# Turning a unit's maxima by four VectorE block transposes in place of one TensorE transpose

## The chip, the core and the metric

The kernel runs on one core of a Trainium2 chip. The core has a matrix engine (TensorE, "PE" in the profile, whose weight loads are listed apart as "PEld"), three engines for elementwise work (VectorE "DVE", ScalarE "ACT", GpSimd "POOL") and SyncE ("SP"), which here only issues transfers. Each engine runs its own list of instructions in order and waits on semaphores for the others. The metric is the time of one execution in microseconds (us) on the device; the kernel before takes 3283.42 us in the median of three runs.

## The reference

One transformer block with normalisation ahead of each half, on an input `x` of 2 x 1024 tokens of width 1024, with 32 heads of 32 and a gated network of inner width 2752, all in float32:

```python
x = x + attn(layernorm(x))
x = x + ffn(layernorm(x))

def attn(x):
    qkv = (x @ attn_qkvw + attn_qkvb).reshape(B, S, 3, HEADS, hd)
    q, k, v = ...                                  # each (B, HEADS, S, hd)
    scores = einsum('bhqd,bhkd->bhqk', q, k) / sqrt(hd)
    ctx = einsum('bhqk,bhkd->bhqd', softmax(scores, axis=-1), v)
    return ctx.transpose(0, 2, 1, 3).reshape(B, S, H) @ attn_ow + attn_ob

def ffn(x):
    return (silu(x @ W_gate.T) * (x @ W_up.T)) @ W_down.T
```

The part that matters here is the softmax: before the exponential, the maximum over all keys is subtracted for each head and each query.

## The kernel before, in words

The work is cut in four blocks: two batches by two halves of 512 query tokens. A block is done in this order: projections of q, k and v (L370, L432), attention, the output projection (`po`, L780), the second normalisation with its transposes (L258), the gated network (products `p`, L922, and `pd`, L1071 and L998; both by seven products on sums of quarters in place of eight, the sums of weights being made once on POOL, L1184).

Attention is cut in 64 units, 16 a block, each of two heads. A unit's scores are 8 tiles (`kt`) of 128 keys by 2 x 512 queries, made two at a time by `scores` (L510) into a PSUM tag "s" with two buffers. ScalarE copies each tile to SBUF (L529) and VectorE takes the running elementwise maximum `top` over the tiles (L526). When the last tile is through, `maximum` brings the 128 partitions of `top` to one value for each column:

- `half(s)`, twice (due 4600 and 6400 after the last scores): VectorE transposes 512 columns of `top` in blocks of 32x32 into `m` (L549) and takes the maximum over each block's rows (L550) into 16 columns of `part`. After it, partition 32a+i, column b of `part` holds the maximum of column 32b+i over the a-th group of 32 partitions. `part` is one tile of 128x128, of which only 32 columns are ever written; it is set to 0 at the start (L463).
- `turn` (due 10500): TensorE transposes all of `part` into a PSUM tile `top` of the tag "lin" (L564), and VectorE reduces the four groups of its first 32 partitions to `neg`, negated (L565).
- `neg` (32x32) is written to memory by SyncE (L570, due 12000) and read back by all 128 partitions into `m` (L573, due 14500).

Later steps add `m` to each tile of scores (`less_maximum`, L580, on POOL, and on VectorE for a quarter of the tiles of the first block), take the exponential on ScalarE (L589), add pairs of tiles (L603, on VectorE and POOL) and multiply with the values on TensorE (`acc`, L618).

The PSUM tag "lin" has three buffers, used in turn by every projection, every transpose of L258, the products of the network, and the `top` of L564. A buffer is free again when VectorE or ScalarE has read it: for `pd` that is L1084 (added to `x`), for `p` the small operations of L936 to L949, for `po` L792.

The order of instructions is written by the program, not by a scheduler. `Emitter.run` walks two lists: `fill`, which holds the projections and the network, with a cost in nanoseconds for each matmul (`MM4` = 855), and `paced`, which holds the attention's steps as evenly spaced beats. A clock is advanced by each step's cost. `em.later(delay, fn)` puts a step off until that clock has passed the present value by `delay`; it is then emitted at once, on whichever engine it names. So a due time sets the place of an instruction in its engine's list, not the moment at which it runs.

Of the kernel before, what the change touches and what calls it, by code (L numbers as in the profile page):

```python
# [9 lines left out]
F32 = mybir.dt.float32  # L10
F32R = mybir.dt.float32r
AF = mybir.ActivationFunctionType
ALU = mybir.AluOpType
AX = mybir.AxisListType

P = 128
HEADS = 32
HD = 32
# [112 lines left out]
def preln_block_kernel(  # L131
# [14 lines left out]
    nc = tc.nc  # L146
# [11 lines left out]
    HPG = P // HD  # L158
# [8 lines left out]
    const = ctx.enter_context(tc.tile_pool(name="const", bufs=1))  # L167
# [29 lines left out]
    def lps(name, shape=(P, NH)):  # L197
        return psum.tile(list(shape), F32, tag="lin", bufs=3, name=name)

    def small(shape, tag, bufs, name):  # L200
        return const.tile(shape, F32, tag=tag, bufs=bufs, name=name)

    ident = const.tile([P, P], F32, tag="ident", name="ident")
# [25 lines left out]
    em = Emitter()  # L229
# [229 lines left out]
    NQ = NH // 2  # L459


    part = const.tile([P, P], F32, tag="part", name="part")
    nc.vector.memset(part, 0.0)  # L463

    class Unit:

# [75 lines left out]
        def maximum(self):  # L542

            n = HD // NS
            self.m = att.tile([P, S], F32, tag="m", bufs=2, name=f"m_{self.name}")

            def half(s):
                cols = slice(s * NH, (s + 1) * NH)
                nc.vector.transpose(self.m[:, cols], self.top[:, cols])  # L549
                nc.vector.tensor_reduce(  # L550
                    part[:, s * n : (s + 1) * n],
                    self.m[:, cols].rearrange("p (b j) -> p b j", j=HD),
                    AX.X,
                    ALU.max,
                )

            for s in range(NS):
                em.later(4600.0 + 1800.0 * s, lambda s=s: half(s))
            d2 = dram.tile([S], F32, tag="d2", bufs=3, name=f"d2_{self.name}")
            neg = small([HD, HD], "neg", 1, f"neg_{self.name}")  # L560

            def turn():
                pt = lps(f"top_{self.name}", (P, P))
                nc.tensor.transpose(pt, part, ident)  # L564
                nc.vector.tensor_reduce(  # L565
                    neg, pt[:HD, :].rearrange("b (a i) -> b i a", i=HD), AX.X, ALU.max, negate=True
                )

            em.later(10500.0, turn)
            em.later(12000.0, lambda: nc.sync.dma_start(d2.rearrange("(b i) -> b i", i=HD), neg))  # L570
            em.later(
                14500.0,
                lambda: nc.sync.dma_start(self.m, d2.partition_broadcast(P)),  # L573
                ("max", self.n),
            )
# [777 lines left out]
```

## Time and profile before

| what | us |
|---|---|
| median of three runs | 3283.42 (3279.31 to 3285.41) |
| profiled execution | 3281.96 |
| its span, first to last instruction | 3280.2 |
| TensorE's granted clock, mean over the span | 0.994 of full |
| VectorE's L526, the running maximum, busy | 545.4 in 448 instructions |
| POOL's L580, subtraction of the maximum, busy | 1180.8 in 480 |
| TensorE's L922, products `p`, busy | 1091.3 in 4704 |
| TensorE's L1071, products `pd`, busy (its larger group) | 442.3 in 960 |

A group of the profile is one line's instructions on one engine: "out<-in" names the tiles by the program's names, "x64" the number, then the busy time in us, the mean of one in ns, and how long the engine stood idle just before them and what ended that. A float32 matmul shows as two records, a transpose as one. A wait "A <- B" is idle time of A ended by B. In a table of stretches of time, each engine has its busy time and count, then come the granted clock, the share in which the DMA engines were busy, and GB/s.

### The profile page before, as it was taken

How to read it: one execution, taken by the hardware profiler on the slowest of the kernel's cores; microseconds unless marked ns; L12 is line 12 of the kernel's file. 1: busy time of each engine (PE TensorE's matmuls, PEld its weight loads, DVE VectorE, ACT ScalarE, POOL GpSimd, SP SyncE). 2: the span in 40 equal slices, each digit the busy share in tenths (PEclk: the TensorE clock that was granted, in tenths of full speed). 3: DMA queues.
4: the chain of work that ended last, by engine and by line, in shares of the span. 5: the costliest groups of instructions: out<-in, count | busy, mean ns of one | idle time of the engine just before them, and what ended most of it. 6: DMA issues, size and time to landing. Idle time of an engine off the chain costs nothing. (4 is left out here: it accounts for less than half of the span.)

```text
span 3280.2 us, 43732 instructions
## 1 busy us (share of the span) xinstructions
PE 3217.5 (98%) x16320; PEld 1801.1 (55%) x16320; DVE 1920.4 (59%) x2478; ACT 1431.2 (44%) x1570; POOL 1758.6 (54%) x871
## 2 busy tenths in 40 slices
PE   8999999999999999999999999989999999999999
PEld 4444444444347655663466556634655566477775
DVE  2265676666356766666666666676666664344334
ACT  2244554444455545563655455545555554010000
POOL 0267776876676655568665555667765665200000
PEclk9999999999999999999999999999999999999999
DMA  4556766655534445446344444463444444544442
GB/s 155 171 184 193 226 192 203 200 180 161 158 99 135 142 151 146 146 146 200 107 142 145 139 141 137 145 192 110 137 145 146 146 138 140 184 151 153 153 152 97
DMA packets 337826, 507.29 MB, mean 155 GB/s; under 512 B 105424, under 2 KB 122064, under 8 KB 337616
## 3 DMA queue, kind: packets, MB, share of 16 engines
q1 hardware_dynamic: 281424, 405.91, 40.3%
q10 hardware_dynamic: 56192, 98.60, 9.8%
q8 instruction: 130, 2.13, 0.3%
q14 instruction: 80, 0.66, 0.1%
HBM read 429.14 MB, written 75.24 MB: 154 GB/s over the span
## 5 line engine op out<-in xcount | busy, mean ns | idle before, releaser
L580 POOL TENSOR_TENSOR p<-p,m 128x1024 f32<-128x1024 f32 x480 | 1180.8, 2483 | 13.6 <-DMA m<-d 13.4
L529 ACT COPY p<-s 128x1024 f32<-128x1024 f32 x512 | 516.7, 1011 | 872.1 <-DVE top L526 664.5
L526 DVE TENSOR_TENSOR top<-s,top 128x1024 f32<-128x1024 f32 x384 | 468.1, 1219 | 289.0 <-PE s L510 280.0
L589 ACT ACTIVATE p<-p 128x1024 f32<-128x1024 f32 x512 | 532.2, 1057 | 234.7 <-POOL p L580 206.8
L922 PE MATMUL p<-sum,m 128*128 128x256 f32 x2688 | 617.8, 383 | 4.9 <-DVE sum L904 3.3
L603 POOL TENSOR_TENSOR p<-p,p 128x1024 f32<-128x1024 f32 x96 | 227.2, 2367 | 658.9 <-ACT p L589 598.3
L922 PEld LDWEIGHTS p<-sum,m 128*128 128x128 f32 x2688 | 503.2, 190 | 124.7 <-issue 43.0
L922 PE MATMUL p<-xn2T,m 128*128 128x256 f32 x2016 | 473.5, 384 | 1.9 <-ACT gate L934 1.3
L370 PE MATMUL pq<-xnT,wqk 128*128 128x512 f32 x1024 | 463.7, 601 | 0.0
L1071 PE MATMUL pd<-wp,h 128*128 128x512 f32 x960 | 442.3, 607 | 8.3 <-DVE x L1084 6.4
L922 PEld LDWEIGHTS p<-xn2T,m 128*128 128x128 f32 x2016 | 378.2, 191 | 98.5 <-issue 45.4
L603 DVE TENSOR_TENSOR p<-p,p 128x1024 f32<-128x1024 f32 x192 | 306.2, 1595 | 134.1 <-ACT p L589 134.0
L370 PEld LDWEIGHTS pq<-xnT,wqk 128*128 128x128 f32 x1024 | 187.2, 190 | 252.8 <-issue 249.0
L1071 PEld LDWEIGHTS pd<-wp,h 128*128 128x128 f32 x960 | 179.3, 193 | 242.5 <-issue 203.4
L510 PE MATMUL s<-q,k 32*128 32x512 f32 x2048 | 300.8, 645 | 7.1 <-ACT p L529 7.0
L1084 DVE TENSOR_TENSOR x<-pd,x 128x512 f32<-128x512 f32 x360 | 236.9, 681 | 86.8 <-PE pd L1071 86.7
L618 PE MATMUL acc<-p,vals 128*32 128x256 f32 x4096 | 266.0, 383 | 1.8 <-DVE p L603 1.8
L1184 POOL TENSOR_TENSOR ws<-raw 128x512 f32<-128x512 f32 x62 | 93.7, 1512 | 299.9 <-DMA raw<-in_w_gu 170.5
L432 PE MATMUL pvv<-wv,xnT 128*128 128x512 f32 x512 | 233.3, 600 | 1.5 <-ACT xnT L266 1.5
L780 PE MATMUL po<-wo,ctx 128*128 128x512 f32 x512 | 234.6, 607 | 0.0
L618 PEld LDWEIGHTS acc<-p,vals 128*32 128x32 f32 x4096 | 120.1, 110 | 143.6 <-issue 70.2
L950 ACT ACTIVATE gate<-gate 128x512 f32<-128x512 f32 x84 | 52.9, 630 | 278.4 <-DVE gate L949 278.0
(96 smaller groups left out, 2451.3 us busy)
## 6 DMA issues: line engine op xcount, KB each, us to landing
m<-dws SPq DMA_DIRECT2D x336, 256.0 KB
m<-in_w_gu SPq DMA_DIRECT2D x252, 256.0 KB
wp<-ddn SPq DMA_DIRECT2D x160, 256.0 KB
m<-d SPq DMA_DIRECT2D x64, 512.0 KB
wp<-in_w_dn SPq DMA_DIRECT2D x120, 256.0 KB
raw<-in_w_gu ACTq DMA_DIRECT2D x84, 256.0 KB
dws<-ws ACTq DMA_DIRECT2D x84, 256.0 KB
x<-in_x SPq DMA_DIRECT2D x32, 512.0 KB
```

The costliest lines, as they stand in the source:

```text
L370: nc.tensor.matmul(ps, wqk[b, g, w, hk][:, k, :], xnT[b, s][:, kc, :], start=(kc == 0), stop=(kc == KC - 1),)
L510: nc.tensor.matmul(ps[a][:, h * NH : (h + 1) * NH], self.k[rows, i * P : (i + 1) * P], self.q[rows, :], start=True, stop=True,)
L526: nc.vector.tensor_tensor(self.top, s, self.p[0] if kt == 1 else self.top, ALU.max)
L529: nc.scalar.copy(self.p[kt], s)
L580: eng.tensor_tensor(p, p, self.m, ALU.add)
L589: nc.scalar.activation(self.p[kt], self.p[kt], AF.Exp, scale=SCALE)
L603: eng.tensor_tensor(self.p[kt], self.p[kt], self.p[kt - back], ALU.add)
L618: nc.tensor.matmul(self.acc[j * HD : (j + 1) * HD, c : c + NQ], w(h), self.p[kt][:, q0 : q0 + NQ], start=start, stop=stop, skip_group_chec ...
L780: nc.tensor.matmul(st["ps"], ctxT[b, blk][:, g, t * P : (t + 1) * P], st["w"][hf, g], start=(g == 0), stop=(g == G - 1),)
L922: nc.tensor.matmul(ps, mats[c, n][:, kc, :], rhs, start=(kc == 0), stop=(kc == hk - 1),)
L1071: nc.tensor.matmul(st["pd"], lefts[n](pi)[:, j, t * P : (t + 1) * P], st["wp", pi, n, j], start=(j == 0), stop=(j == PART // 2 - 1),)
L1084: nc.vector.tensor_tensor(xs, st["pd"], xs, op)
```

## The change

`part` shrinks from 128x128 to the 32 columns that are written, and is no longer set to 0. In `turn`, TensorE's transpose into PSUM goes; VectorE instead transposes each of the four 32x32 groups of `part` into its place in a new SBUF tile `turned` (32 partitions, 4 x 32), and the reduction reads that. `turn` is due at 8200 instead of 10500. The reduction's result, its write and its read back, and their due times, are the same.

```diff
-    part = const.tile([P, P], F32, tag="part", name="part")
-    nc.vector.memset(part, 0.0)
+    part = const.tile([P, HD], F32, tag="part", name="part")
...
+            turned = small([HD, HPG, HD], "turned", 1, f"turned_{self.name}")
+
             def turn():
-                pt = lps(f"top_{self.name}", (P, P))
-                nc.tensor.transpose(pt, part, ident)
+                for a in range(HPG):
+                    nc.vector.transpose(turned[:, a, :], part[a * HD : (a + 1) * HD, :])
                 nc.vector.tensor_reduce(
-                    neg, pt[:HD, :].rearrange("b (a i) -> b i a", i=HD), AX.X, ALU.max, negate=True
+                    neg, turned.rearrange("b a i -> b i a"), AX.X, ALU.max, negate=True
                 )
 
-            em.later(10500.0, turn)
+            em.later(8200.0, turn)
```

In the built program, the lists of TensorE (apart from the 64 transposes), ScalarE, POOL and SyncE are the same as before, instruction for instruction. On VectorE, the four transposes and the reduction stand directly behind the second `part` of L550 or up to three instructions later; before, the reduction stood one to four instructions behind it in all but five units.

## The prediction

> **What bounds the kernel now.** First the busy shares, to see which engine sets the time.
>
> ```profile
> PE 3217.5 (98%) x16320; PEld 1801.1 (55%) x16320; DVE 1920.4 (59%) x2478; ACT 1431.2 (44%) x1570; POOL 1758.6 (54%) x871
> ```
>
> TensorE (PE) is busy for 98% of the span of 3280.2 us, and the next engine, VectorE (DVE), for 59%. So an edit is worth what it takes from PE's own work, or from the 62.7 us (3280.2 - 3217.5) in which PE stood still; work moved to DVE costs only where DVE is late for PE. Second, the transpose that the change removes, by its line, L564.
>
> ```profile
> L564 PEld LDWEIGHTS top<-ident,part x64: 137/140/183, 126.7 to 2730.8; 128*128 128x128 f32 x64
> L564 PE MATMUL top<-ident,part x64: 272/273/474, 127.2 to 2731.1; 128*128 128x128 f32 x64
> ...
>   DVE part L550: 37.4, 22
> ...
>   DVE neg L565: 38.4, 22
> ```
>
> There are 64, one a unit. PE and its weight load together stood idle 37.4 us for `part` just before it, and in turn DVE's next step, `neg`, stood idle 38.4 us for it: a ping-pong between two engines that both run their queues in order. Third, PE's own waits.
>
> ```profile
> PE top L564 <- DVE part L550: 16.1, 10, 3.0
> PE pt_a L258 <- ACT x L247: 10.2, 4, 7.8
> PE pd L1071 <- DVE x L1084: 7.1, 12, 1.4
> ```
>
> The largest wait of all that PE has is the one that the change takes away.
>
> **The change part by part.** *a) The 64 transposes on PE.* A record lasts 273 ns, but matmuls are pipelined, so its price is how much later the next matmul starts. Where nothing waits, the timeline gives it:
>
> ```profile
> 2728.47 2.75 PE L922 MATMUL p<-xn2T,m 128*128 128x256 f32 x12
> ...
> 2731.06 0.27 PE L564 MATMUL top<-ident,part 128*128 128x128 f32 x1
> ...
> 2731.17 2.75 PE L922 MATMUL p<-xn2T,m 128*128 128x256 f32 x12
> ```
>
> The next matmul starts 0.11 us after it (2731.17 - 2731.06); read at 45 undisturbed places it is 0.109. 64 x 0.109 = 7.0 us, all on the path. The weight load (140 ns) lies under the matmul before.
>
> *b) PE's wait for `part`.* At 19 of the 64 places the start of the matmul in front of the transpose and that of the one behind it lie further apart than their usual distance (0.216 us after L922, 0.429 after L1071, 0.52 after the scores) plus 0.109. Summed over the timeline this excess is 28.0 us; the largest are 3.8 at 2031, 3.3 at 982, 3.1 at 1821, 3.0 at 2203 and 2.7 at 1534. How much comes back depends on what PE needs next. One place:
>
> ```profile
> 1817.97 1.28 DVE L1084 TENSOR_TENSOR x<-pd,x 128x512 f32<-128x512 f32 x2
> 1819.17 0.70 DVE L549 STREAM_TRANSPOSE m<-top 128x512 f32<-128x512 f32 x1
> 1819.90 0.69 DVE L550 TENSOR_REDUCE part<-m 128x16 f32<-128x512 f32 x1
> 1820.51 1.28 DVE L1084 TENSOR_TENSOR x<-pd,x 128x512 f32<-128x512 f32 x2
> ...
> 1824.04 0.27 DVE L565 TENSOR_REDUCE neg<-top 32x32 f32<-32x128 f32 x1
> ```
>
> ```profile
> 1817.47 1.14 PE L510 MATMUL s<-q,k 32*128 32x512 f32 x8
> 1820.64 0.33 PE L564 MATMUL top<-ident,part 128*128 128x128 f32 x1 [2.03 <-DVE part L550]
> 1821.84 5.12 PE L1071 MATMUL pd<-wp,h 128*128 128x512 f32 x8 [0.87 <-DVE x L1084]
> ```
>
> PE ends the scores at 1818.61, stands until 1820.64 for `part`, and then 0.87 us more, since its next product needs one of the three `lin` PSUM buffers and the transpose took the one that came free first. Without the transpose the product takes that one, free at 1819.25 (1817.97 + 1.28), so it could start 2.59 us earlier (1821.84 - 1819.25) of the 3.1 lost. I read this slack (start of a product less the end of the eviction three products before, transposes not counted) at all 19 places for the next four products: where it is the smaller, it replaces the wait. That leaves 23.8 of 28.0 us.
>
> *c) DVE's new work.* Four block transposes of 32x32 and the reduction, now out of SBUF, replace one reduction. No 32x32 transpose is in the trace; the nearest rows are
>
> ```profile
> L549 DVE STREAM_TRANSPOSE m<-top 128x512 f32<-128x512 f32 x128 | 89.9, 702 | 1.8
> L550 DVE TENSOR_REDUCE part<-m 128x16 f32<-128x512 f32 x128 | 87.8, 686 | 4.4
> ...
> L565 DVE TENSOR_REDUCE neg<-top 32x32 f32<-32x128 f32 x64 | 17.4, 272 | 38.6 <-PE top L564 38.4
> ...
> L243 DVE RECIPROCAL rstd_f<-sd_f 128x1 f32<-128x1 f32 x16 | 2.6, 164 | 10.3 <-ACT sd_f L241 10.3
> ```
>
> The two reductions give (686 - 272) / (512 - 128) = 1.08 ns an element above 134 ns, so 32 elements are 168 ns, and with the 16 ns by which a transpose exceeds a reduction of 512, about 0.18 us. The bounds are 0.044 (702 x 32 / 512, no fixed part) and 0.70 (no saving for a small one); 0.18 is nearest to the one-element operation's 0.164. Four are 0.72, the reduction 0.27, with one gap for dependent steps (0.03 after L549 above) 1.0 us a unit, against 0.27. Over the span DVE gains 64 x 0.75 = 48 us of work and loses 38.4 of waiting.
>
> DVE instructions that start back to back overlap: two L1084 of 0.68 take 1.28. The Trainium skill ("VectorE: DVE Perf Modes", section "Two Vector instructions with no wait between them") holds an instruction until the earlier ones have finished if its input starts in another quadrant of partitions than the last one's, as these four do; by it there is no overlap, as I took it; with overlap of 0.08 each a unit would cost 0.3 us less, at most 19 x 0.3 = 6 us of this sum. No row here shows it.
>
> *d) What is queued behind.* The steps are emitted earlier (due 8200 instead of 10500), so DVE runs them ahead of one to three instructions that stood between `part` and `neg`: in 63 units the add of L603, in some the evictions L1084 or L936 to L952. These come up to 1.0 us later, and PE waits for the evictions. The slack behind the transpose is 1.9 us or more at nearly every undisturbed unit (2.8 is usual in L922 stretches; over 12 before 880 us), so 1.0 is hidden there by PE's next products; without that cover it would be up to 46 x 1.0 us (the units from 890 us on). At the 19 places I take the full 1.0 from the slack: 17 us of b) stay. The scores' PSUM (7 us or more of slack at the first scores after the transpose in most units) and the add's users (median 16 us) are clear. On SyncE the write of `neg` (L570) keeps its place and due time; in 28 units it waited for `neg`, and loads queue behind it, so earlier can only help. POOL and ACT issue what they did. The memset of `part` (165 ns, at the start) is beside PE's wait for the first input.
>
> *e) The clock.* Behind the longest of these waits the granted clock is halved:
>
> ```profile
> 1821.32:1824.73 3.41, 2.89 (x4) 1.34 (x5) 3.25 (x6) 0.00 (x0) 0.00 (x0) 0.50 0.02 7
> ...
> 2203.61:2207.03 3.42, 3.42 (x10) 0.91 (x7) 1.93 (x3) 1.01 (x1) 3.22 (x1) 0.50 0.94 264
> ```
>
> The column with 0.50 is the clock. There are nine such stretches between 800 and 2300 us, and six begin in this wait or within 2.2 us behind its end (982, 1534, 1821, 1947, 2033, 2203; waits of 1.6 to 3.0 us). In those six, the steps between matmuls of one line are longer than usual by 8.5 us in all. With d) some 1 to 2 us of wait remains at three of the six, so I take 5 us (bounds 0 and 8.5). The Trainium skill ("TensorE: Matmul & The Clock Gate", section "HAM oscillation — how this bites in real kernels") asks only that idle gaps stay below about 3.4 us; by that none of these waits would lower the clock and the forecast would be 5 us longer. The trace disagrees: 1.62 us before 1946.9 was enough.
>
> *Sum.* 7.0 + 17 + 5 = 29 us. The profiled execution took 3281.96 us (span 3280.2 and 1.8 around it), 1.46 below the median of 3283.42, so 3253 for such an execution and **3254** on the median's scale.
>
> **The rivals.** *The wait only moves.* DVE is late for reasons of its own (between 1816.6 and 1824.5 it has no idle time), and PE waits at the next eviction instead. For it: weight loads of L1071 wait 34.5 us, 52 times, for L1084. Against: the slack of 1.9 to 2.6 us that the freed buffer gives. Then only a) remains: 3283.4 - 7.0 = 3276.
>
> *DVE becomes the limit: slower.* If a 32x32 transpose costs what L549 does, the turn is 4 x 0.70 + 0.27 = 3.1 us, and evictions behind it come 1.2 us past a slack of 1.9 in the 46 units from 890 us on: 55 us lost, against 7.0 and some 7 of the waits whose slack exceeds 3.1: 3283 + 41 = 3324. It decides from about 2.3 us a turn (46 x 0.4 = 18 us lost, against 7 and about 11), half a microsecond a transpose. Against: one-element and 12-element operations at 164 to 209 ns. In this sense the Trainium skill speaks against the change: "VectorE: DVE Perf Modes", section "Rules for kernel authors", gives a 128x128 transpose to TensorE and only a 32x32 one to DVE, and here four of the latter replace one of the former; the removed step needed only 32 columns of it, and by that rule's other row DVE is the right place.
>
> *Nothing comes of it.* What PE saves returns as waits for another chain, such as ACT's copies of the scores (L529; PE waited 7.0 us for them, and two halved stretches stand behind such waits): 3283. Against: the median slack of the scores' buffers, 5.5 us.
>
> **How the numbers follow.** Forecast (gain of 17 to 43 us, 3240 to 3266) 0.66; the wait moves 0.14; nothing 0.07; slower 0.09; a larger gain, by halved stretches vanishing elsewhere too, 0.04. The upper bound of the gain is 7.0 + 28.0 + 8.5 = 43.5, or 3240, and 2 for the scatter of single times gives the low end, 3238. The high end takes in the moved wait (3276) and 3 us of late evictions: 3279. A change under 0.2% (6.6 us) can't be told from none. Faster: 0.66 + 0.04 + two thirds of 0.14 = 0.79; within: the rest and 0.07, 0.11; slower 0.10.
>
> **What would show it.** a) No `top` record on PE, 64 matmuls fewer. b) PE idle falls from 62.7 to below 45 us, and the products behind 1818 and 2028 start some 1.5 to 2.6 us earlier after the scores. c) 32x32 transposes of 0.15 to 0.22 us, DVE busy near 1970 us, `neg` without idle time before it. d) Waits of PE and of weight loads for L1084 not above the present 7.1 and 34.5 us by more than 5. e) Halved stretches at 1534, 2203 and 982 gone or shorter. Transposes above 0.5 us, or L1084 in the place of `part` among PE's waits, would make the forecast wrong.

## The result, and the profile after

The changed kernel took 3267.21 us in the median of four executions, beside 3284.39 us for the kernel before: a ratio of 0.9954 (95% interval 0.9941 to 0.9967). Two later repeats, beside their own runs of the kernel before, gave ratios of 0.9950 (0.9938 to 0.9962) and 0.9953 (0.9940 to 0.9966). So it is faster by some 0.48% (by the mean of the three ratios, 0.9952), 16 us; 29 were forecast. The profiled execution was one of its fastest, 3264.24 us with a span of 3262.5.

The busy shares of the changed kernel, as in the first fence of the prediction:

```profile
PE 3206.8 (98%) x16256; PEld 1792.5 (55%) x16256; DVE 1999.2 (61%) x2733; ACT 1432.7 (44%) x1570; POOL 1767.8 (54%) x871
```

PE has its 64 records fewer, but it still stands still for 55.7 us (3262.5 - 3206.8), against 62.7. DVE's busy time grew by 79 us. The new steps, by their lines (least, median and longest in ns):

```profile
L566 DVE STREAM_TRANSPOSE turned<-part x256: 189/199/204, 122.6 to 2711.4; 32x32 f32<-32x32 f32 x128
```

```profile
L567 DVE TENSOR_REDUCE neg<-turned x64: 355/364/381, 123.5 to 2711.7; 32x32 f32<-32x128 f32 x64
```

Nothing waits before either of them. PE's own waits, longest first (total, times, longest):

```profile
PE s L509 <- ACT p L528: 10.5, 5, 3.9
PE pt_a L258 <- ACT x L247: 10.1, 4, 7.8
PE pd L1073 <- DVE x L1086: 9.9, 13, 1.9
PE acc L620 <- DVE p L605: 5.4, 3, 2.1
```

The wait for `part` is gone. In its place are longer waits for three things that other engines make: ACT's copies of the scores, DVE's evictions of `pd` (7.1 us before), and DVE's adds of the probabilities, which the products with the values (`acc`) read. The copies and the adds in the kernel before:

```profile
PE s L510 <- ACT p L529: 7.0, 5, 2.6
...
PE acc L618 <- DVE p L603: 1.8, 2, 1.5
```

The lines of the changed kernel are shifted by up to two: L1073 is L1071 of before, L605 is L603.

At the place that the prediction worked through, 1821 us before, the changed kernel does what was expected:

```profile
1812.34 1.28 DVE L1086 TENSOR_TENSOR x<-pd,x 128x512 f32<-128x512 f32 x2
1813.53 0.70 DVE L548 STREAM_TRANSPOSE m<-top 128x512 f32<-128x512 f32 x1
1814.27 0.69 DVE L549 TENSOR_REDUCE part<-m 128x16 f32<-128x512 f32 x1
...
1816.66 0.84 DVE L566 STREAM_TRANSPOSE turned<-part 32x32 f32<-32x32 f32 x4
1817.53 0.36 DVE L567 TENSOR_REDUCE neg<-turned 32x32 f32<-32x128 f32 x1
```

```profile
1811.81 1.14 PE L509 MATMUL s<-q,k 32*128 32x512 f32 x8
1813.67 1.98 PE L1073 MATMUL pd<-wp,h 128*128 128x512 f32 x4 [0.72 <-DVE x L1086]
```

The product starts 1.86 us after the scores' first record (1813.67 - 1811.81), where it was 4.37 us before (1821.84 - 1817.47): 2.51 us earlier, of 2.59 read from the buffers. In two more traces of the changed kernel it is 1.91 and 2.49.

**Where the gain is, and where it went.** Apart from the 64 transposes, the matmuls of both kernels are the same and in the same order, so each can be matched with itself, and the step from one to the next compared. Three sums come out: at the 19 places where PE had waited in the trace of before, at the other 45 places of the removed transpose, and everywhere else (us, positive is gained, against the profiled execution of before).

| profiled execution | 19 places | other 45 | elsewhere | in all |
|---|---|---|---|---|
| changed kernel, first | 26.7 | 5.3 | -14.3 | 17.7 |
| changed kernel, second (`again`) | 27.6 | 5.3 | -24.1 | 8.8 |
| changed kernel, third (`base`) | 26.8 | 5.3 | -19.4 | 12.7 |
| no block transposes (`no_blocks`) | 28.4 | 5.3 | -7.9 | 25.9 |
| no turn at all (`no_turn`) | 28.9 | 5.3 | -4.2 | 30.0 |

What was to be earned at the places of the transpose was earned, nearly all of it. Between 14 and 24 us were given back elsewhere. The last two rows are experiments, described below. The steps elsewhere can be split by the matmul that came later (us, the changed kernel as the mean of its three traces):

| steps elsewhere to | changed kernel | `no_turn` |
|---|---|---|
| scores (PE waits there for ACT's copies) | -5.7 | -6.1 |
| products with the values (for DVE's adds) | -6.3 | -2.5 |
| `pd` (for DVE's evictions) | -4.0 | +0.9 |
| any matmul while the clock is halved in either trace | -1.9 | +2.4 |
| all others | -1.3 | +1.0 |

So of the 15 us between the two columns 13 stand at the adds, the evictions and the clock. The loss at the scores is there without VectorE's turn too, so the turn does not explain it; from trace to trace it is 3.3 to 7.9 us, and what makes ACT's copies come late was not tried.

One place of the second row, 4 to 6 us behind a place where 2.67 us were gained (1534 us before):

```profile
1527.50 10.31 POOL L582 TENSOR_TENSOR p<-p,m 128x1024 f32<-128x1024 f32 x4
...
1531.61 1.07 PE L620 MATMUL acc<-p,vals 128*32 128x256 f32 x16
1531.87 0.84 DVE L566 STREAM_TRANSPOSE turned<-part 32x32 f32<-32x32 f32 x4
...
1532.75 0.38 DVE L567 TENSOR_REDUCE neg<-turned 32x32 f32<-32x128 f32 x1
...
1533.06 2.53 DVE L605 TENSOR_TENSOR p<-p,p 128x1024 f32<-128x1024 f32 x1
...
1535.64 0.64 PE L620 MATMUL acc<-p,vals 128*32 128x256 f32 x8 [2.10 <-DVE p L605]
```

The same add before, and the products of which the second half read it:

```profile
1533.45 1.49 DVE L603 TENSOR_TENSOR p<-p,p 128x1024 f32<-128x1024 f32 x1
...
1538.90 1.04 PE L618 MATMUL acc<-p,vals 128*32 128x256 f32 x16
```

There the add came ahead of the reduction and was done at 1534.94, some 4 us ahead of those products. Now PE comes to them earlier; the add comes later, since the turn stands in front of it, and it takes 1.0 us longer. PE waits 2.10 us, and the granted clock (the last column but two in this table of stretches) drops right behind:

```profile
1530.00:1536.20 6.20, 4.09 (x54) 1.62 (x50) 6.06 (x10) 2.91 (x3) 6.20 (x3) 1.00 0.97 278
1536.20:1539.60 3.40, 3.40 (x15) 1.21 (x8) 0.52 (x1) 2.84 (x3) 1.61 (x1) 0.50 1.03 297
```

### The profile page after: what moved, and what is told of

It is laid out like the page before. It is cut to its first block, busy times and chain, and to the rows that moved or that the text cites. A ratio compares the mean times of both kernels' runs of the same rounds, so it can differ in the third digit from the quotient of the medians.

```text
span 3262.5 us, 43853 instructions
## 1 busy us (share of the span) xinstructions
PE 3206.8 (98%) x16256; PEld 1792.5 (55%) x16256; DVE 1999.2 (61%) x2733; ACT 1432.7 (44%) x1570; POOL 1767.8 (54%) x871
## 4 chain that ended last, share of the span: by engine, by line
PE 86%; DVE 6%; DMA 3%; POOL 2%; issue 1%; ACT 1%; SPq 0%; ACTq 0%; POOLq 0%; DVEq 0%
PE p L924 31%; PE pq L370 11%; PE pd L1073 11%; PE acc L620 9%; PE s L509 7%; PE pvv L432 7%; PE po L782 7%; DVE top L525 1%; DVE x L1086 1%; POOL p L582 1%; DMA ctx<-dctx 1%; DMA rec<-drec 1%; PE pg L968 1%; PE pd L1000 1%; DVE p L605 1%
## 5 line engine op out<-in xcount | busy, mean ns | idle before, releaser
L582 POOL TENSOR_TENSOR p<-p,m 128x1024 f32<-128x1024 f32 x480 | 1193.3, 2508 | 11.5 <-DVE top L525 8.4
L605 POOL TENSOR_TENSOR p<-p,p 128x1024 f32<-128x1024 f32 x96 | 227.1, 2366 | 629.7 <-ACT p L591 595.6
L1073 PE MATMUL pd<-wp,h 128*128 128x512 f32 x960 | 438.0, 602 | 10.3 <-DVE x L1086 9.9
L605 DVE TENSOR_TENSOR p<-p,p 128x1024 f32<-128x1024 f32 x192 | 335.7, 1748 | 135.5 <-ACT p L591 134.8
L1073 PEld LDWEIGHTS pd<-wp,h 128*128 128x128 f32 x960 | 177.1, 190 | 248.1 <-issue 200.0
L509 PE MATMUL s<-q,k 32*128 32x512 f32 x2048 | 302.2, 643 | 10.6 <-ACT p L528 10.5
```

Source lines behind the costliest of these rows:

```text
L509: nc.tensor.matmul(ps[a][:, h * NH : (h + 1) * NH], self.k[rows, i * P : (i + 1) * P], self.q[rows, :], start=True, stop=True,)
L582: eng.tensor_tensor(p, p, self.m, ALU.add)
L605: eng.tensor_tensor(self.p[kt], self.p[kt], self.p[kt - back], ALU.add)
L1073: nc.tensor.matmul(st["pd"], lefts[n](pi)[:, j, t * P : (t + 1) * P], st["wp", pi, n, j], start=(j == 0), stop=(j == PART // 2 - 1),)
```

## The experiments

Ratios are to runs of the kernel before on the same chip and at the same time; the kernels that share a section below don't all share those.

| run | ratio, 95% interval | median, us | before, us |
|---|---|---|---|
| again | 0.9950, 0.9938 to 0.9962 | 3269.0 | 3285.3 |
| late | 0.9960, 0.9945 to 0.9975 | 3271.7 | 3285.3 |
| pe_early | 1.0180, 1.0161 to 1.0200 | 3347.3 | 3285.3 |
| spare | 1.0040, 1.0026 to 1.0054 | 3301.1 | 3285.3 |
| no_part | 0.9980, 0.9969 to 0.9991 | 3276.0 | 3282.7 |
| no_blocks | 0.9941, 0.9923 to 0.9960 | 3260.3 | 3282.7 |
| double | 0.9994, 0.9980 to 1.0008 | 3280.2 | 3282.7 |
| no_turn | 0.9914, 0.9896 to 0.9931 | 3252.3 | 3282.7 |
| double_first | 0.9970, 0.9961 to 0.9980 | 3273.2 | 3285.1 |
| double_rest | 0.9980, 0.9971 to 0.9990 | 3278.1 | 3285.1 |
| blocks_too | 1.0061, 1.0048 to 1.0075 | 3303.9 | 3285.1 |
| by_dma | 1.0105, 1.0091 to 1.0118 | 3318.3 | 3285.1 |
| base | 0.9953, 0.9940 to 0.9966 | 3268.6 | 3284.3 |
| by_act | 0.9953, 0.9939 to 0.9966 | 3267.0 | 3284.3 |
| beat_more | 1.0010, 0.9999 to 1.0021 | 3287.6 | 3284.3 |
| vals3 | 0.9959, 0.9946 to 0.9972 | 3269.9 | 3284.0 |
| beat_vals | 0.9962, 0.9949 to 0.9976 | 3273.7 | 3284.0 |

### Is it the order? again, late, pe_early

The first suspicion was the place above: the turn, due earlier, stands in front of the add.

> The changed kernel itself, once more, beside the next three on one chip. Both theories: 15 to 19 us faster than the kernel before (ratio 0.9942 to 0.9955). In the records, if the loss at 1534, 2209 and 982 us belongs to the order of instructions and not to one execution, PE again waits about 2 us for the add L605 at the first two and about 2.4 us for L833 at the third; the loss of some 3 us near 892 us (a late landing of rec, behind which ACT's copies come late) may be absent if it was of one execution.

> Only the due time of the turn is put back, 8200 to 10500, so that VectorE's order is that of the kernel before, with four block transposes more. Theory A (the place of the turn gives the gain back): ahead of the adds it makes PE wait for L605 at about 1534 and 2209 us (2.3 us each, and a halved stretch of the clock of 1.5 us behind each) and for L833 near 988 us (3 us); with the turn behind them these go, and it is about 10 us faster than the changed kernel, 3257 us. Theory B (VectorE's added work gives it back, wherever it stands, 0.8 to 1.2 us a unit): within 2 us of the changed kernel, with the same waits on other lines.

```diff
-            em.later(8200.0, turn)
+            em.later(10500.0, turn)
```

`again` repeats the changed kernel: the same time, and PE again waits for L605 (6.4 us in 5 waits) and for L833, one of DVE's sums of quarters (2.4 us). `late` is not faster (0.9960 beside 0.9950, with intervals that overlap), so theory A fell: with the turn behind the adds, the wait for L833 is 1.2 us, but PE waits for L605 no less, 8.4 us in 7 waits.

> The kernel before with its TensorE transpose, but the turn due at 8200: the move alone. Theory A: PE comes to the transpose 2.3 us earlier in its list and finds part less often ready; its idle time before the transpose grows from 37 us to over 60, and the kernel is 5 to 25 us slower than before. Rival: the earlier place itself brings the gain of the change; then 5 us or more faster than before.

```diff
 # the kernel before
-            em.later(10500.0, turn)
+            em.later(8200.0, turn)
```

Slower by 1.8%, far more than expected. The waits of PE for `part` in it:

```profile
PE top L564 <- DVE part L550: 72.4, 29, 5.4
```

They were 16.1 us in 10 waits. The place matters greatly where PE makes the transpose, and not measurably where DVE makes it.

### What was PE's transpose worth? spare, no_part

> The changed kernel with one more TensorE transpose a unit, of the identity, at the old place, into a lin PSUM buffer that nothing reads: it waits for no part, but takes its slot on PE and a turn of the three buffers. If a slot costs 0.109 us and the buffers do not matter: 7.0 us slower than the changed kernel. If the buffer's turn matters as much as I read at 1821 and 2031 us (1.3 us at each of some ten places): 15 to 20 us slower.

```diff
+            def spare():
+                pt = lps(f"spare_{self.name}", (P, P))
+                nc.tensor.transpose(pt, ident, ident)
+
             em.later(8200.0, turn)
+            em.later(10500.0, spare)
```

A transpose that waits for no maxima makes the changed kernel 32 us slower (3301.1 beside 3269.0), more than either forecast; 7 of them are its slots. Besides its slot it takes one of the three "lin" buffers for a turn, and PE's waits for the evictions of `pd` grow from 9.9 to 22.6 us:

```profile
PE pd L1078 <- DVE x L1091: 22.6, 22, 2.5
PE acc L625 <- DVE p L610: 11.6, 6, 4.1
```

The waits for the adds grow too (5.4 before). Why they do, with nothing changed on DVE, is not shown.

> The kernel before, but its transpose turns the identity in place of part, so it doesn't wait for VectorE's maxima; it still takes its slot on PE and a turn of the three lin buffers, and VectorE still reads the result. neg is then not the maximum. If the wait for part is what the change was mainly paid for (17 to 28 us of the sum of the prediction): 3257 to 3268 us. If the slot and the buffer's turn are (the run spare: 32 us for both): within 10 us of the kernel before, 3275 to 3285.

```diff
 # the kernel before
-                nc.tensor.transpose(pt, part, ident)
+                nc.tensor.transpose(pt, ident, ident)
```

Without the wait for `part`, but with the slot and the buffer, the kernel before gains only 7 us. PE's waits in it:

```profile
PE pd L1071 <- DVE x L1084: 12.9, 15, 2.2
...
PE acc L618 <- DVE p L603: 6.6, 5, 2.5
```

At the 19 places only 10.9 us come back of 28 (26.7 in the changed kernel). At 1821 and 1947 us nothing comes back: there PE had waited for `part`, and now waits for a buffer in its place. The wait for `part` and the buffer's turn limit the same stretches side by side, and only taking away both pays. The sum of the prediction had this right, for it read the slack with the buffer given back.

### What does VectorE's turn cost? no_blocks, no_turn, double, blocks_too

> The changed kernel without the four block transposes; the reduction reads a tile that was set to 0 once, so neg is 0. If VectorE's added work gives back some 15 us, the four transposes being 0.84 of its 1.1 us a unit: 8 to 15 us faster than the changed kernel, 3254 to 3261 us. If its work is hidden, as the prediction took it but for the 19 places: within 4 us of the changed kernel.

```diff
+    turned = const.tile([HD, HPG, HD], F32, tag="turned", name="turned")
+    nc.vector.memset(turned, 0.0)
...
-                for a in range(HPG):
-                    nc.vector.transpose(turned[:, a, :], part[a * HD : (a + 1) * HD, :])
```

> The changed kernel without the turn at all: no block transposes and no reduction after them, neg set to 0 once and written out as before. It gives the price of all that VectorE does for the turn, 1.2 us a unit. If that gives back what the removal of PE's transpose earned: 15 us or more faster than the changed kernel, 3247 to 3254 us. If it is hidden: 3263 to 3269 us.

```diff
+    neg = const.tile([HD, HD], F32, tag="neg", name="neg")
+    nc.vector.memset(neg, 0.0)
...
-            def turn():
-                for a in range(HPG):
-                    nc.vector.transpose(turned[:, a, :], part[a * HD : (a + 1) * HD, :])
-                nc.vector.tensor_reduce(neg, ...)
-            em.later(8200.0, turn)
```

> The changed kernel with each of the block transposes made twice, 0.84 us more of VectorE a unit in the same place. If VectorE's work in this place costs PE in proportion: 8 to 15 us slower than the changed kernel, 3277 to 3284 us. If it is hidden: within 4 us.

```diff
-                for a in range(HPG):
+                for a in [*range(HPG), *range(HPG)]:
```

Without the turn it is 16 us faster than the changed kernel by the medians and 12 by the ratios, and with its block transposes doubled 12 and 14 us slower. Both intervals lie clear of the changed kernel's. `no_blocks` lies between (8 us faster by the medians, 4 by the ratios), but its interval overlaps with the changed kernel's. So the turn, 1.23 us of DVE a unit (0.84 + 0.36 and the gap), costs 0.2 to 0.25 us a unit of PE's time. In `no_turn` the write of `neg` also waits for no maxima; POOL's waits for `m` are 2.2 us there, beside 3.0, 10.5 and 10.4 in the three traces of the changed kernel, and what that gave is not separated. `double` needs no such allowance. PE's waits for DVE in `no_turn`, then in `double`:

```profile
PE acc L609 <- DVE p L594: 3.8, 4, 2.3
...
PE pd L1062 <- DVE x L1075: 3.1, 8, 0.6
```

```profile
PE acc L620 <- DVE p L605: 13.7, 10, 4.9
PE pd L1073 <- DVE x L1086: 11.0, 13, 1.4
```

The two together are 6.9 us without the turn, 15.3, 15.8 and 20.2 in the three traces of the changed kernel, and 24.7 with twice the block transposes. DVE had time to spare on the average (61% busy), but PE waits at moments, and each 0.8 us more makes some of them later.

> The kernel before, with the four block transposes in addition (their result is not used), due 8200: VectorE's added work alone, PE's transpose left. If the two parts of the change add up (31 us off PE, 15 back by VectorE): 12 to 18 us slower than before, 3295 to 3301. If VectorE's work costs more beside PE's transpose, since part and the evictions come later for a PE that waits for both: over 20 us slower.

```diff
 # the kernel before
+            def blocks():
+                for a in range(HPG):
+                    nc.vector.transpose(turned[:, a, :], part[a * HD : (a + 1) * HD, :HD])
+
+            em.later(8200.0, blocks)
             em.later(10500.0, turn)
```

19 us slower. With the others it fills a table (medians, us):

| | PE's transpose of `part` | PE's transpose of the identity | none |
|---|---|---|---|
| DVE without the blocks | 3284 (before) | 3276 (no_part) | 3260 (no_blocks) |
| DVE with the blocks | 3304 (blocks_too) | 3301 (spare) | 3268 (changed) |

The four blocks cost 4 to 8 us where PE makes no transpose, a size that is not clear of the noise, and 19 to 25 where one takes a buffer. The transpose costs 24 us without the blocks and 36 with them. The two parts of the change are not a sum of two prices. (The middle column is not quite one kernel: in `no_part` VectorE reads the transpose's result, in `spare` nothing does.)

### In which units? double_first, double_rest

> The changed kernel with each block transpose made twice in the 16 units of the first block alone (up to about 890 us), where the products' buffers had 12 us and more of slack. If VectorE's time costs PE only where buffers or sums come late for it: within 3 us of the changed kernel (3268). If each unit pays alike: a quarter of the 12 us of the run double, 3 us, and the same again for a noisy measure; more than 6 us would say that the first block pays most.

> The same in the 48 units of the other blocks alone, where the evictions of pd and the adds are what PE waits for. If the cost is there: 9 to 13 us slower than the changed kernel, 3277 to 3281 us. If not: within 4 us.

```diff
 def turn():
+    twice = 2 if self.phase == 0 else 1      # double_first; double_rest: self.phase > 0
-    for a in range(HPG):
+    for a in [*range(HPG)] * twice:
```

By the ratios, beside the mean of the three measures of the changed kernel (0.9952): 6 us in the first block's 16 units, 9 us in the other 48. The turns of the first block's units end at 740 us, not at 890. For the first block the price is above the 3 us of both forecasts, though the interval still overlaps, barely, with the changed kernel's three. There the product buffers have 12 us of slack by the prediction's reading; what PE waits for is the adds: between 60 and 870 us PE's waits for L605 come to 3.7 us in `double_first`, 3.0 in `double`, 0.4 in `no_turn`, and none, 0.8 and 1.7 in the three traces of the changed kernel. In the first block DVE makes three adds for each four tiles, in the others one. So its lateness can come through `acc` there, but 2 to 4 us of these waits are not all of the 6.

### Can the turn be had for less? by_dma, by_act

> The changed kernel with one block transpose of all 128 partitions (0.2 us) in place of four of 32, and four small transfers that bring its groups side by side; the reduction is due 11500. VectorE has 0.6 us less a unit. If its time is what gives the gain back: 5 to 9 us faster than the changed kernel, 3259 to 3263 us. If the transfers come late or hold SyncE's queue: as fast or slower, with waits for the loads.

```diff
-                for a in range(HPG):
-                    nc.vector.transpose(turned[:, a, :], part[a * HD : (a + 1) * HD, :])
...
-            em.later(8200.0, turn)
+            em.later(8200.0, lambda: nc.vector.transpose(blocks, part))
+            em.later(8400.0, gather)       # 4 x nc.sync.dma_start(turned[:, a, :], blocks[32a : 32a + 32, :])
+            em.later(11500.0, turn)        # the reduction
```

> The changed kernel with one block transpose of all 128 partitions on VectorE (0.2 us) and four small copies on ScalarE that bring its groups into one, the reduction due 11000. VectorE has 0.64 us less a unit, ScalarE some 1 us more, of which it has idle time. If VectorE's time is what gives the gain back (8 us for the 0.84 us of the run no_blocks): 4 to 8 us faster than base. If the reduction now waits for ScalarE, as it did for the transfers of by_dma: no faster than base, with idle time of VectorE before neg.

```diff
-                for a in range(HPG):
-                    nc.vector.transpose(turned[:, a, :], part[a * HD : (a + 1) * HD, :])
...
-            em.later(8200.0, turn)
+            em.later(8200.0, lambda: nc.vector.transpose(blocks, part))
+            em.later(8300.0, gather)       # 4 x nc.scalar.copy(turned[:, a, :], blocks[32a : 32a + 32, :])
+            em.later(11000.0, turn)
```

Neither is faster than the changed kernel. By transfers it is 50 us slower: in most units the reduction starts 3.7 to 7.3 us after the block transpose, in six 10 to 18 us after it, and DVE stands in front of the reduction:

```profile
DVE neg L566 <- DMA turned<-blocks: 159.7, 53, 12.0
...
PE s L509 <- ACT p L528: 51.1, 12, 10.5
```

By ScalarE it is as fast as `base`. DVE is relieved of 0.64 us a unit (one block transpose of 128x32 takes 0.206 us), but ScalarE, which runs in order too, stands for the block transpose, and DVE in six units for ScalarE's copies:

```profile
ACT turned L572 <- DVE blocks L574: 117.8, 44, 7.1
...
DVE neg L566 <- ACT turned L572: 14.9, 6, 6.3
```

That this standing is what uses up the relief is not shown: PE's waits for ACT's copies of the scores are 7.2 us in this trace and 9.8 in that of `base`.

> The changed kernel once more, as the measure for the next two: 3266 to 3272 us.

### Adds or evictions? beat_more, vals3, beat_vals

> The changed kernel with the values' products one beat (about 2.5 us) later, so that the adds of L605 may come later without PE waiting for them. If the adds are where VectorE's lateness reaches PE: PE's waits for L605 (5 to 6 us) go and it is 3 to 8 us faster than base. If the evictions are: within 3 us of base. The probabilities' ring keeps its 19 tiles, so ScalarE may come to wait for PE to free them; then it is slower.

```diff
-        for n in range(total + NT + LAG + 3):
+        for n in range(total + NT + LAG + 4):
...
-            k, kt = divmod(n - NT - LAG - 3, NT)
+            k, kt = divmod(n - NT - LAG - 4, NT)
```

Inconclusive: the waits for the adds were gone, but PE waited 23.0 us for the values' load. A unit's last products were now emitted behind the load of the unit after next into the same one of two buffers, so this kernel multiplies them with that unit's values. A third buffer mends that:

> The changed kernel with three buffers for a unit's values in place of two, nothing else: within 3 us of the changed kernel, 3266 to 3272 us.

> The same with the values' products one beat later. If VectorE's lateness reaches PE by the adds, PE's waits for L605 (5 to 10 us in the changed kernel) go and it is 4 to 10 us faster than vals3. If by the evictions, the waits for L1086 stay and it is within 3 us of vals3. If the probabilities' ring is now too short, ScalarE waits for PE before L528, and it is slower.

```diff
-    vals = [const.tile(...) for i in range(2)]
+    vals = [const.tile(...) for i in range(3)]
...
-            self.v = vals[n % 2]
+            self.v = vals[n % 3]
```

`beat_vals` is as fast as `vals3`. PE has no wait for the adds any more; its waits for the evictions are double. `vals3`, then `beat_vals`:

```profile
PE pd L1073 <- DVE x L1086: 12.0, 15, 1.9
...
PE acc L620 <- DVE p L605: 5.6, 3, 2.7
```

```profile
PE pd L1073 <- DVE x L1086: 24.6, 26, 3.5
```

So taking away the waits for the adds did not bring their time back: as far as this pair shows, DVE is behind, and PE meets it at the next thing it needs. (Moving the products by a beat also changes what stands between the evictions, which this pair does not separate.) No version faster than the changed kernel that still takes the maxima was found.

## Why the prediction was right and wrong

The direction held, and the time lies inside the outer range (3238 to 3279), but above the 3240 to 3266 us that the forecast itself was given; the gain was about half of what was forecast. What the prediction said of PE's side held. What it said of VectorE's side, that the new work is hidden, did not.

*a) The slots: right.* At the 45 undisturbed places the step from one matmul to the next is shorter by 0.12 us in the mean, 5.3 us in all there.

*b) The waits for `part`: right, and more than was kept.* Of 28.0 us, 23.8 were read as recoverable and 17 kept. Measured at the 19 places: 26.7 to 27.6 us, less 19 x 0.109 = 2.1 for the slots, so about 25, or 8 more than the sum had. The deduction of 1.0 us from the slack for DVE's new work was hardly needed there: without the turn the 19 places give 28.9. This is how far the reading of buffers carries: 1.91 to 2.51 us at 1821 us, of 2.59. (The 37.4 us read at L564 counts PE and its weight load for the same stretches; PE alone stood 16.1 us. The sum went by the 28.0 us of the steps, so nothing hangs on it.)

*c) DVE's new steps: near.* A block transpose took 0.199 us, 0.18 forecast (0.044 and 0.70 were the bounds). The four take 0.84 us together. With an overlap of 0.08 they would take 0.56, so they don't overlap; the rule of the Trainium skill that was cited ("VectorE: DVE Perf Modes", section "Two Vector instructions with no wait between them") agrees. The reduction out of SBUF took 0.364 us, not 0.272 as out of PSUM. In all 1.23 us a unit against 1.0.

*d) This is the step that failed*: "The slack behind the transpose is 1.9 us or more at nearly every undisturbed unit ..., so 1.0 is hidden there by PE's next products", and "the add's users (median 16 us) are clear". The term elsewhere was put at 0; it measured -14 to -24 us in three traces, -4 in the trace without the turn. So DVE's work costs 10 to 20 us of PE's time by the traces, 12 to 16 by the ratios and the medians of `no_turn` and the changed kernel. PE's idle time fell to 55.7 us, not below 45. Two faults lie in the step. Only the next four products behind the transpose were read, not the values' products between them and not later units. And the adds were cleared by a median, where the tail decides: by the same reading the smallest slacks in the trace of before were 0.05, 0.06, 0.3 and 0.4 us, and of 512 tiles some 30 were below 2.5. The median was also taken over too much: 16 us is that of all 512 tiles, half of which wait for no add. Over the 160 that one of DVE's adds finishes last it is 5.1 us, and all that were below 2.5 are among them. Besides, PE spends part of what it gains by coming earlier to the same late adds: behind the place at 1534 us, where it gained 2.67 us, it stood 2.10. (The units from 890 us on are 45 by their transposes, not 46; that changes none of the bounds by more than 1.2 us.)

*e) The clock: the stretches named went, others came.* Those at 1821, 1947 and 2033 us are absent in all three traces of the changed kernel. A halved stretch stands behind the wait for the add at 1536 to 1543 us in all three, the one at 982 us comes at 989 to 990 us in two, and there are new ones at 468 (two) and at 1651 to 1652 us (two). Lost at half rate (half of the time of such stretches) were 22.2 us before, and 14.2, 22.0 and 18.9 in the three; the 5 us forecast are 3.8 in the mean, with a spread of 0.2 to 8.0, so the term is not measured. The rule of the Trainium skill ("TensorE: Matmul & The Clock Gate", section "HAM oscillation — how this bites in real kernels"), idle gaps below 3.4 us, is again not enough: in the changed kernel the wait of 2.10 us up to 1535.64 was followed by a halved clock at 1536.2.

In the mean of the three traces the sum is 27.0 at the 19 places and 5.3 at the others, less 19.3 elsewhere, 13 us, against an execution of before that was itself 2.4 us below its median; that makes 15.4, beside the 16 us of the ratios. The term of -19.3, the clock's stretches among it, stood in the prediction as the 5 us gained by the clock. That the total still came to half of the forecast is luck in part: 8 us too few at the 19 places stand against 24 too many elsewhere.

Of the rivals, "the wait only moves" is half right: PE's waits for the evictions grew from 7.1 to 9.9 us (weight loads: 34.5 to 41.3, more than the 5 us allowed for), but by DVE's work, not at once behind the removed wait. That DVE becomes the limit decided at 2.3 us a turn by the estimate; `double`, with 2.1 us, is at 0.9994 (0.9980 to 1.0008) of the kernel before, so the break-even point is there. That the two numbers meet is luck: by the estimate a delay below 1.9 us costs nothing but at the 19 places, and in the runs 12 to 16 us are lost at 1.23 us and about as much again with 0.84 more. "Nothing comes of it" named ACT's copies of the scores as the next wait, and against it stood their median slack of 5.5 us; this rival is right for the 5.7 us at the scores (6.1 without the turn).

## What to carry to other kernels

Moving work off the engine that is busy all the time pays for its slot, for the wait in front of it and for the buffer that it takes; here the slot and the wait alone were worth some 7 us each, and the rest came only with the buffer. The engine that takes the work over is not free merely because it is busy for only 60% of the time: if it hands results to the first engine at many places, look at the tail of the slack at every such place, and test the price by doubling the new work. Here a time gained at one wait was partly spent at the next meeting with a late engine, so the sum of the gains at single places was more than the kernel gained.

## What was not expected of the hardware

DVE's adds (two inputs in SBUF) grew slower in every run without PE's wait for `part`, from 1.595 us in the mean to 1.67 to 1.81, with nothing changed in them. The group before and after, out of the lists by line:

```profile
L603 DVE TENSOR_TENSOR p<-p,p 128x1024 f32<-128x1024 f32 x192 | 306.2, 1595 | 134.1 <-ACT p L589 134.0
```

```profile
L605 DVE TENSOR_TENSOR p<-p,p 128x1024 f32<-128x1024 f32 x192 | 335.7, 1748 | 135.5 <-ACT p L591 134.8
```

That is 29 of the 79 us by which DVE's busy time grew. The traces show where it comes from. Of the 192 adds, 86 before and 75 after lie clear of POOL's two-input operations, and these take 1.23 us at most in every run. Those during which POOL runs such operations all the time are 54 before and 64 after; they take 1.2 to 3.4 us, in the mean 1.89 before and 2.01 after. The one-input transposes of L549 (L548 after) take 0.70 us with POOL at work and without. So the adds are slow where they meet POOL's work, and in the changed kernel they meet it more often. No run takes POOL's work away by itself to try it, and why they meet more often is not shown.
